# One image's sampling interleaved with the other images' offsets stage, and the whole depthwise convolution as diagonal matmuls

## Chip, cores and metric

The kernel runs on one core of a Trainium2 chip, in float32 throughout. The metric is device time in microseconds. The engines are PE (TensorE matmul; PEld its weight loads), DVE (VectorE), ACT (ScalarE), POOL (GpSimd), and SP, whose queue issues most DMAs.

## The reference

Four images of 64 x 64 positions and 256 channels go through two layers: a deformable convolution (DCNv3 style), and then an additive attention with a routed feed-forward part. Only the first layer touches the change. Cut to what matters:

```python
x1 = lax.conv_general_dilated(x1, dw_k, (1, 1), [(1, 1), (1, 1)], feature_group_count=C)  # depthwise 3x3
x1 = silu(bn(x1))
offset = x1 @ off_w + off_b                       # 8 groups x 9 points x 2
mask = softmax((x1 @ mask_w + mask_b).reshape(N, H, W, G, P), -1)
xp = x @ in_w + in_b                              # the projection that is sampled
# bilinear samples of the padded xp at (position + point + offset), times mask, summed over the 9 points
out = (samples * m).sum(-1) @ out_w + out_b
x = x + out                                       # then attention and feed-forward over the tokens
```

Its input is `_gn(x)`, a group norm with 32 groups over one image, so an image has to be read whole before its convolution can start.

## The kernel before

It works in float32, in these stages, one after the other:

1. `offsets_and_weights` for all four images (called with slabs of 8 token tiles, 8 x 128 tokens, and two row buffers). Per image: `front` loads the image in eight pieces (`xt`), transposes them on PE so that channels lie on partitions, takes statistics on DVE (L332), copies to `xn` on ACT (L333), forms the group statistics through two tiny matmuls, and normalises `xn` in two ACT instructions (L357), one for each half of the channels. Then, slab by slab:
   - `convolution(s)`: the depthwise 3x3. Channel half 1 is nine matmuls with diagonal matrices `diag`, accumulated in PSUM (L411), then SiLU on ACT (L415). Channel half 0 is one multiply and eight multiply-adds on DVE (L423, L425), then SiLU (L426). It is written one slab ahead.
   - `taps(s)`: the matmuls to offsets and mask logits (L435), the bias on DVE into `raw` (L439), the softmax's maximum, subtraction and exponential (L447 to L449).
   - `window(s)`: the softmax's rest, `raw` stored, hat functions of the offsets on ACT (L464 to L468), and from these a 5 x 5 window of weights `w5` for each position and group, built on DVE (L474, L477, L479). It is transposed on PE (L488), copied (L490) and stored to `wt_d` (L492).
   - `projection(i)`: 16 image rows of the sampled projection (L378, L383), stored as rows (`xp_d`, L389) and, transposed (L396, L397), as a table (`tab_d`, L398).

   The `front` of the next image is drawn on between the slabs; `xn` has two buffers.
2. The zero borders of `xp_d` and `tab_d`: one zeroed tile, 24 DMAs on SP (L1306, L1307).
3. `sample_image(0, 6)`: the sampling of image 0 as a dense sum over the 5 x 5 window: for each of 4 chunks of 1024 tokens, 2 channel halves and 25 displacements, a DMA that broadcasts the weights `wb` (L668, 2 x depth buffers), a product on DVE (L677), an accumulation on DVE (L684); then the output projection on PE (L696) with two adds (L700, L703). Ahead of it `list_tokens` lists the tokens whose offsets leave the window, and `exact_rows` does up to 128 of these by gathers (L611, L622, L623), a step of it beside every product.
4. Then for each image the attention, preceded by `attention_prep` (and the feed-forward part of the image before); `sample_image(n + 1)` runs beside the attention of image n. A last feed-forward ends the kernel.

A list scheduler orders the instructions of each engine, in the order of the program where several are ready. `keep(...)` pins an instruction behind everything traced before it on its engine; the products and accumulations of the sampling are pinned. `pinned` is a stand-in for `nc.vector` that pins every instruction. `offsets_and_weights` uses plain `nc.vector`.

Both `offsets_and_weights` and `sample_image` can be generators: the latter yields after every product and every accumulation, which is called a step here.

Of the kernel before, what the change touches and what calls it, by code (L numbers as in the profile page):

```python
# [9 lines left out]
F32 = mybir.dt.float32  # L10
# [6 lines left out]
P = 128  # L17
# [9 lines left out]
MP = 68  # L27
# [17 lines left out]
def layers_kernel(ctx: ExitStack, tc: tile.TileContext, a, out: bass.AP):  # L45
# [208 lines left out]
    def offsets_and_weights(images, slab, rows_bufs):  # L254

        ca = S.a_one
        inw = load_const(ca, "inw", [P, CC, C], a["L0_conv_in_w"].rearrange("(k p) f -> p k f", p=P))
# [50 lines left out]

        diag = ca.tile([P, K2, P], F32, name="diag")
        for tap in range(K2):  # L310
            nc.vector.tensor_scalar(diag[:, tap], ident, dwk[:, 1, tap : tap + 1], None, ALU.mult)

        def front(n):

            xn = S.a_xn.tile([P, CC, PITCH, PITCH], F32, tag="xn", name="xn")
            for k in range(CC):
                for e in (0, PITCH - 1):
                    nc.gpsimd.memset(xn[:, k, e, :], 0.0)
                    nc.gpsimd.memset(xn[:, k, :, e : e + 1], 0.0)

            st = S.a_sm.tile([P, CC, 8, 6], F32, tag="st", name="st")
            for s in range(8):
                xt = S.a_ld.tile([P, 4, C], F32, tag="xt", name="xt")
                nc.sync.dma_start(
                    out=xt, in_=x_d[n, s * 512 : (s + 1) * 512].rearrange("(t p) c -> p t c", p=P)
                )
                for k in range(CC):
                    pt = S.a_t.tile([P, 4, P], F32, tag="pt", name="pt")
                    for t in range(4):
                        nc.tensor.transpose(pt[:, t, :], xt[:, t, k * P : (k + 1) * P], ident)  # L330
                    ptf = pt.rearrange("p t q -> p (t q)")
                    nc.vector.bn_stats(st[:, k, s, :], ptf)  # L332
                    nc.scalar.copy(  # L333
                        xn[:, k, 1 + 8 * s : 9 + 8 * s, 1 : 1 + W],
                        ptf.rearrange("p (r w) -> p r w", w=W),
                    )
                yield
            mv = S.a_sm.tile([P, CC, 2], F32, tag="mv", name="mv")
            for k in range(CC):
                nc.vector.bn_aggr(mv[:, k, :], st[:, k].rearrange("p s f -> p (s f)"))  # L340
# [5 lines left out]
            nc.vector.tensor_copy(gm, pg)  # L346
            gv = S.a_sm.tile([P, CC], F32, tag="gv", name="gv")
            nc.vector.tensor_sub(gv, mv[:, :, 0], gm)
            nc.vector.tensor_mul(gv, gv, gv)
            nc.vector.tensor_add(gv, gv, mv[:, :, 1])  # L350
# [3 lines left out]
            nc.vector.scalar_tensor_tensor(gm, gm, -1.0, gr, ALU.mult, ALU.mult)  # L354
            for k in range(CC):
                inner = xn[:, k, 1 : 1 + H, 1 : 1 + W]
                nc.scalar.activation(inner, inner, AF.Identity, bias=gm[:, k : k + 1], scale=gr[:, k : k + 1])  # L357
            xns[n] = xn

        images = list(images)  # L360
        xns = {}
        for _ in front(images[0]):
            pass
        for at, n in enumerate(images):
            xn = xns.pop(n)
            after = front(images[at + 1]) if at + 1 < len(images) else iter(())


# [34 lines left out]
            def convolution(s):  # L403
                x1 = S.a_wk.tile([P, CC, slab * P], F32, tag="x1", name="x1")
                x1s[s] = x1
                r0 = 2 * slab * s
                for o in range(0, slab * P, 512):
                    pc = S.a_m.tile([P, 8, W], F32, tag="pm", name="pc")
                    for tap in range(K2):
                        r = r0 + o // W + tap // 3  # L410
                        nc.tensor.matmul(  # L411
                            pc, diag[:, tap], xn[:, 1, r : r + 8, tap % 3 : tap % 3 + W],
                            start=(tap == 0), stop=(tap == K2 - 1),
                        )
                    nc.scalar.activation(  # L415
                        x1[:, 1, o : o + 512], pc.rearrange("p r w -> p (r w)"), AF.Silu,
                        bias=bnsh[:, 1:2], scale=bns[:, 1:2],
                    )
                acc = x1[:, 0].rearrange("p (r w) -> p r w", w=W)
                for tap in range(K2):  # L420
                    src = xn[:, 0, r0 + tap // 3 : r0 + tap // 3 + 2 * slab, tap % 3 : tap % 3 + W]
                    if tap == 0:
                        nc.vector.tensor_scalar(acc, src, dwk[:, 0, 0:1], None, ALU.mult)  # L423
                    else:
                        nc.vector.scalar_tensor_tensor(acc, src, dwk[:, 0, tap : tap + 1], acc, ALU.mult, ALU.add)  # L425
                nc.scalar.activation(x1[:, 0], x1[:, 0], AF.Silu, bias=bnsh[:, 0:1], scale=bns[:, 0:1])  # L426

            def taps(s):
                x1 = x1s.pop(s)
                raw = S.a_wk.tile([P, slab, 3 * GP], F32, tag="raw", name="raw")  # L430
                for t in range(0, slab, 2):
                    po = S.a_m.tile([P, 2, 3 * GP], F32, tag="pm", name="po")
                    for j in range(2):
                        for k in range(CC):
# [3 lines left out]
                            )  # L438
                    nc.vector.tensor_tensor(  # L439
                        raw[:, t : t + 2, :], po, omb.to_broadcast([P, 2, 3 * GP]), ALU.add  # L440
# [5 lines left out]
                rbc = red.to_broadcast([P, slab, G, K2])  # L446
                nc.vector.tensor_reduce(red, m3, AX.X, ALU.max)  # L447
                nc.vector.tensor_tensor(m3, m3, rbc, ALU.subtract)
                nc.scalar.activation(m3, m3, AF.Exp)  # L449
                raws[s] = raw, m3, red, rbc  # L450

            def window(s):
                raw, m3, red, rbc = raws.pop(s)
                nc.vector.tensor_reduce(red, m3, AX.X, ALU.add)
                nc.vector.reciprocal(red, red)
                nc.vector.tensor_tensor(m3, m3, rbc, ALU.mult)
                nc.sync.dma_start(
# [8 lines left out]
                nc.scalar.activation(hat[:, 1], off, AF.Abs)  # L466
                nc.vector.tensor_reduce(omax[:, n, s * slab : (s + 1) * slab], hat[:, 1], AX.X, ALU.max)
                nc.scalar.activation(hat[:, 1], hat[:, 1], AF.Identity, scale=-1.0, bias=one_c)  # L468
# [3 lines left out]
                for ey in range(3):  # L472
                    my = S.a_w1p.tile([P, slab, GP], F32, tag="my", name="my", bufs=2)
                    nc.vector.tensor_mul(my, raw[:, :, 2 * GP :], hat[:, ey, :, GP:])  # L474
                    for ex in range(3):
                        mxy = S.a_w1p.tile([P, slab, GP], F32, tag="mxy", name="mxy", bufs=2)
                        nc.vector.tensor_mul(mxy, my, hat[:, ex, :, :GP])  # L477
                        blk = w5[:, :, ex : ex + 3, ey : ey + 3]
                        nc.vector.tensor_tensor(  # L479
                            blk, blk, mxy.rearrange("p t (g i j) -> p (t g) i j", i=3, j=3), ALU.add  # L480
                        )
# [14 lines left out]
            for s in range(ns):  # L496
                if s + 1 < ns:
                    convolution(s + 1)
                taps(s)
                window(s)  # L500
                for i in range(s * (H // 16) // ns, (s + 1) * (H // 16) // ns):
                    projection(i)
                for _ in range(8 // ns):
                    next(after, None)
            for _ in after:
                pass

# [874 lines left out]
```

## Time and profile before

| | us |
|---|---|
| median of 3 runs | 11147.51 (11145.21 to 11148.35) |
| profiled execution, its own time | 11148.32 |
| its span | 11146.6 |
| first `xn` normalised from | 52.8 |
| first product of the sampling (L677) | 872.8 |
| first load of tokens for the attention (L742) | 1478.5 |
| DVE, PE, ACT, POOL busy in the whole span | 8634.7, 9316.6, 7435.1, 5068.5 |

The four images' normalisations begin at 52.8, 247.3, 441.1 and 633.3 us. A row of a group of instructions names the line, the engine, the operation, output and inputs, the tile, the count, the busy time and the mean length of one, then the idle time of that engine just before them and what ended it. Matmuls of float32 operands appear as two records each.

### The profile page before, as it was taken

What the parts mean: (1) busy time and instruction counts of PE and PEld (TensorE: products, weight loads), DVE (VectorE), ACT (ScalarE), POOL (GpSimd) and SP (SyncE); (2) the same over time, 40 slices, a digit from 0 to 9 for tenths busy, and PEclk for the clock granted to TensorE, in tenths of its full rate; (3) what the DMA queues carried; (4) which work ended last, traced back from release to release, by engine and by line L of the source; (5) the groups of instructions that cost most, each with busy time, mean ns of one, the idle gap of its engine ahead of it and who ended that gap; (6) DMA issues with size and microseconds to landing.
All of it is one profiled execution on the core that took longest, in us unless ns stands there. A gap on an engine that the chain in (4) does not pass through costs nothing. (4 is left out here: it accounts for less than half of the span.)

```text
span 11146.6 us, 116484 instructions
## 1 busy us (share of the span) xinstructions
PE 9316.6 (84%) x38460; PEld 4513.2 (40%) x38460; DVE 8634.7 (77%) x13490; ACT 7435.1 (67%) x8505; POOL 5068.5 (45%) x2931
## 2 busy tenths in 40 slices
PE   7870049999999489999999489999999499999994
PEld 4540024444444244444444244444444244444443
DVE  7767859899998549899997459899997447777772
ACT  4440027777888437777888447777888369999982
POOL 0005107754445227654445237654445135555552
PEclk8985559999999789999999689999999699999997
DMA  3336622322220213222220222222220200000002
GB/s 113 121 129 196 216 91 76 69 77 70 74 75 29 76 58 77 70 77 69 71 75 22 82 60 79 68 73 73 71 76 13 86 22 6 9 9 7 6 7 70
DMA packets 381684, 766.42 MB, mean 69 GB/s; under 512 B 49072, under 2 KB 212944, under 8 KB 381040
## 3 DMA queue, kind: packets, MB, share of 16 engines
q1 hardware_dynamic: 350896, 712.74, 19.6%
q0 software_dynamic: 30144, 45.87, 2.9%
q8 instruction: 310, 5.08, 0.2%
q14 instruction: 334, 2.74, 0.1%
HBM read 581.28 MB, written 177.14 MB: 68 GB/s over the span
## 5 line engine op out<-in xcount | busy, mean ns | idle before, releaser
L849 PE MATMUL nn<-qn,kf 32*128 32x512 f32 (+1 forms) x12288 | 4688.4, 653 | 192.6 <-DVE r L854 149.1
L854 DVE TENSOR_TENSOR r<-nn,r 128x512 f32<-128x512 f32 x6144 | 3946.3, 683 | 952.5 <-PE nn L849 925.4
L926 POOL TENSOR_TENSOR r<-r 128x1024 f32<-128x1024 f32 x1024 | 2721.3, 2658 | 3191.7 <-DVE r L854 3161.0
L920 ACT ACTIVATE r<-d 128x1024 f32<-128x1024 f32 x3072 | 3116.8, 1015 | 1411.9 <-DVE r L930 917.9
L839 PE MATMUL d<-qf,kf 32*128 32x512 f32 (+1 forms) x12288 | 3404.6, 642 | 51.1 <-ACT r L920 49.9
L922 ACT ACTIVATE r<-r 128x1024 f32<-128x1024 f32 x3072 | 3123.9, 1051 | 32.7
L849 PEld LDWEIGHTS nn<-qn,kf 32*128 32x128 f32 (+1 forms) x12288 | 1444.9, 187 | 2057.5 <-DVE r L854 1645.9
L876 PE MATMUL pv<-v,et 128*128 128x257 f32 x8192 | 2203.2, 414 | 14.7 <-DVE acv L896 14.7
L876 PEld LDWEIGHTS pv<-v,et 128*128 128x128 f32 x8192 | 1576.7, 203 | 1047.6 <-issue 815.6
L839 PEld LDWEIGHTS d<-qf,kf 32*128 32x128 f32 (+1 forms) x12288 | 1027.7, 188 | 1316.3 <-issue 575.2
L928 POOL TENSOR_TENSOR r<-r 128x512 f32<-128x512 f32 x1024 | 1321.4, 1290 | 94.7 <-DVE r L854 16.4
L684 DVE TENSOR_TENSOR ac<-ac,prd 128x1024 f32<-128x1024 f32 x768 | 1008.9, 1314 | 6.2
L677 DVE TENSOR_TENSOR prd<-xs,wb 128x1024 f32<-128x1024 f32 x768 | 980.9, 1277 | 0.0
L611 POOL DMA_INDIRECT ga<-tab,tii x576 | 742.8, 1290 | 240.0 <-issue 121.6
L860 ACT ACTIVATE et<-et,nshift 128x512 f32<-128x512 f32 x1024 | 723.6, 707 | 26.6 <-DVE et L933 26.6
L930 DVE TENSOR_TENSOR r<-r 128x512 f32<-128x512 f32 x1024 | 707.9, 691 | 12.5 <-POOL r L926 12.1
L933 DVE TENSOR_TENSOR et<-r 128x512 f32<-128x512 f32 x1024 | 697.3, 681 | 5.5 <-POOL r L928 5.0
L110 ACT ACT_TABLE_LOAD x9 | 11.5, 1283 | 888.4 <-DVE mv L738 730.0
L696 PE MATMUL pmo<-outwp,ac 128*128 128x256 f32 x512 | 141.4, 427 | 455.3 <-DVE ac L684 407.6
L1239 POOL DMA_INDIRECT sort<-v,rif x128 | 123.0, 961 | 517.3 <-DVE rif L250 360.8
L1131 PE MATMUL pcn<-kpart,ones 128*128 128x15 f32 (+2 forms) x72 | 21.6, 378 | 396.0 <-DVE kjunk L250 212.1
L471 POOL MEMSET w<- 128x1600 f32 x16 | 22.9, 1432 | 678.1 <-PE ptw L488 481.9
(347 smaller groups left out, 5496.1 us busy)
## 6 DMA issues: line engine op xcount, KB each, us to landing
wb<-wt SPq DMA_DIRECT2D x800, 512.0 KB
tab<-tb SPq DMA_DIRECT2D x128, 256.0 KB
v<-t SPq DMA_DIRECT2D x64, 512.0 KB
xs<-xp SPq DMA_DIRECT2D x32, 680.0 KB
xp<-xp SPq DMA_DIRECT2D x32, 544.0 KB
xt<-in_x_dram SPq DMA_DIRECT2D x32, 512.0 KB
xr<-in_x_dram SPq DMA_DIRECT2D x64, 256.0 KB
t<-xr SPq DMA_DIRECT2D x64, 256.0 KB
```

The costliest lines, as they stand in the source:

```text
L611: keep(nc.gpsimd.indirect_dma_start(out=ga[:, s, dy].rearrange("p c e -> p (c e)"), out_offset=None, in_=tab_d[n], in_offset=bass.Indirect ...
L677: keep(nc.vector.tensor_tensor(pr.rearrange("p (r w) -> p r w", w=W), src, wb.rearrange("p (r w) -> p r w", w=W), ALU.mult,))
L684: keep(nc.vector.tensor_add(ac[:, f, :], ac[:, f, :], pr))
L839: keep(nc.tensor.matmul(d[:, j, :], kf[g, blk, rows(kt)], qs[q][0][g, blk, :], start=True, stop=True))
L849: keep(nc.tensor.matmul(nn, kf[g, blk, rows(kt)], qs[q][1][g, blk, :], start=True, stop=True))
L854: keep(nc.vector.tensor_tensor(r[:, j, :], ns[j], r[:, j, :], ALU.mult))
L860: keep(nc.scalar.activation(ets[b], ets[b], AF.Exp, bias=nshift))
L876: keep(nc.tensor.matmul(pv, ets[b0 + i][:, rows(j)], v[:, k0 + i, :], start=(i == 0), stop=(i == PVB - 1)))
L920: keep(nc.scalar.activation(rs[b, p], ds.pop((b, p)), AF.Ln))
L922: keep(nc.scalar.activation(rs[b, p], rs[b, p], AF.Exp, scale=-1.0))
L926: keep(nc.gpsimd.tensor_tensor(rs[b, 1], rs[b, 1], rs[b, 2], ALU.add))
L928: keep(nc.gpsimd.tensor_tensor(rs[b, 1][:, 0], rs[b, 1][:, 0], rs[b, 3][:, 0], ALU.add))
```

## The change

- The zero borders move ahead of everything else and are issued from ACT's queue.
- `offsets_and_weights` becomes a generator with slabs of 4 token tiles instead of 8, one row buffer, one `xn` buffer and fewer `xt`, `tb`, `wT` and PSUM buffers. It runs image 0 by itself up to its first yield. Then the other three images are worked through with their DVE instructions pinned, yielding after each of eight loading steps, after each `taps` and after each slab's `window` and projections, and at each of these yields six steps of `sample_image(0, 2)` are drawn. `sample_image` has a depth of 2 in place of 6: four `wb` buffers in place of twelve, two of the others as before.
- An image's `front` is no longer drawn on beside the slabs of the image before it, but ahead of its own slabs.
- The depthwise convolution of both channel halves is done by diagonal matmuls; `diag` has 18 matrices in place of 9, and L423, L425 and L426 go.

The diff, cut to its core; `vec.` replaces `nc.vector.` in all of `front`, `taps` and `window` in the same manner as in the lines shown:

```diff
-        diag = ca.tile([P, K2, P], F32, name="diag")
-        for tap in range(K2):
-            nc.vector.tensor_scalar(diag[:, tap], ident, dwk[:, 1, tap : tap + 1], None, ALU.mult)
-
-        def front(n):
+        diag = ca.tile([P, CC, K2, P], F32, name="diag")
+        for k in range(CC):
+            for tap in range(K2):
+                nc.vector.tensor_scalar(diag[:, k, tap], ident, dwk[:, k, tap : tap + 1], None, ALU.mult)
+
+        def front(n, vec):
...
-                    nc.vector.bn_stats(st[:, k, s, :], ptf)
+                    vec.bn_stats(st[:, k, s, :], ptf)
...
-        for _ in front(images[0]):
-            pass
-        for at, n in enumerate(images):
+        for n in images:
+            first = n == images[0]
+            vec = nc.vector if first else pinned
+            for _ in front(n, vec):
+                if not first:
+                    yield
             xn = xns.pop(n)
-            after = front(images[at + 1]) if at + 1 < len(images) else iter(())
...
-                for o in range(0, slab * P, 512):
-                    pc = S.a_m.tile([P, 8, W], F32, tag="pm", name="pc")
-                    for tap in range(K2):
-                        r = r0 + o // W + tap // 3
-                        nc.tensor.matmul(
-                            pc, diag[:, tap], xn[:, 1, r : r + 8, tap % 3 : tap % 3 + W],
-                            start=(tap == 0), stop=(tap == K2 - 1),
+                for k in range(CC):
+                    for o in range(0, slab * P, 512):
+                        pc = S.a_m.tile([P, 8, W], F32, tag="pm", name="pc")
+                        for tap in range(K2):
+                            r = r0 + o // W + tap // 3
+                            nc.tensor.matmul(
+                                pc, diag[:, k, tap], xn[:, k, r : r + 8, tap % 3 : tap % 3 + W],
+                                start=(tap == 0), stop=(tap == K2 - 1),
+                            )
+                        nc.scalar.activation(
+                            x1[:, k, o : o + 512], pc.rearrange("p r w -> p (r w)"), AF.Silu,
+                            bias=bnsh[:, k : k + 1], scale=bns[:, k : k + 1],
                         )
...
-                acc = x1[:, 0].rearrange("p (r w) -> p r w", w=W)
-                for tap in range(K2):
-                    src = xn[:, 0, r0 + tap // 3 : r0 + tap // 3 + 2 * slab, tap % 3 : tap % 3 + W]
-                    if tap == 0:
-                        nc.vector.tensor_scalar(acc, src, dwk[:, 0, 0:1], None, ALU.mult)
-                    else:
-                        nc.vector.scalar_tensor_tensor(acc, src, dwk[:, 0, tap : tap + 1], acc, ALU.mult, ALU.add)
-                nc.scalar.activation(x1[:, 0], x1[:, 0], AF.Silu, bias=bnsh[:, 0:1], scale=bns[:, 0:1])
...
                 taps(s)
+                if not first:
+                    yield
                 window(s)
                 for i in range(s * (H // 16) // ns, (s + 1) * (H // 16) // ns):
                     projection(i)
-                for _ in range(8 // ns):
-                    next(after, None)
-            for _ in after:
-                pass
+                if not first:
+                    yield
+            if first:
+                yield
...
-    with scope(
-        ("a_one", 1, 0), ("a_xn", 2, 0), ("a_ld", 3, 0), ("a_wk", 2, 0), ("a_w1p", 1, 0), ("a_sm", 2, 0),
-        ("a_t", 4, 1), ("a_m", 4, 1),
-    ):
-        offsets_and_weights(range(NB), SLAB, 2)
...
-                    nc.sync.dma_start(out=xp_d[n][f][:, q0 : q0 + 2 * MP], in_=zm[:, : 2 * MP])
-                nc.sync.dma_start(
+                    nc.scalar.dma_start(out=xp_d[n][f][:, q0 : q0 + 2 * MP], in_=zm[:, : 2 * MP])
+                nc.scalar.dma_start(
                     out=tabw[q0 : q0 + 2 * MP].rearrange("(p r) c -> p (r c)", r=2), in_=zm[:MP]
                 )
...
-    with scope(("two", 2, 0), ("sb", 2, 0), ("dn", 1, 0), ("ps_m", 2, 1)):
-        for _ in sample_image(0, 6):
+    with scope(
+        ("a_one", 1, 0), ("a_xn", 1, 0), ("a_ld", 2, 0), ("a_wk", 2, 0), ("a_w1p", 1, 0), ("a_sm", 2, 0),
+        ("two", 2, 0), ("sb", 2, 0), ("dn", 1, 0), ("a_t", 3, 1), ("a_m", 3, 1), ("ps_m", 2, 1),
+    ):
+        others = offsets_and_weights(range(NB), SLAB // 2, 1)
+        next(others)
+        first = sample_image(0, 2)
+        for _ in others:
+            for _ in range(6):
+                next(first, None)
+        for _ in first:
             pass
```

More of the change, by code (lines that the diff above doesn't have):

```diff
@@ L339, in front @@
             for k in range(CC):
-                nc.vector.bn_aggr(mv[:, k, :], st[:, k].rearrange("p s f -> p (s f)"))
+                vec.bn_aggr(mv[:, k, :], st[:, k].rearrange("p s f -> p (s f)"))
             gavgf = gavg.rearrange("p a b -> p (a b)")
@@ L345, in front @@
             gm = S.a_sm.tile([P, CC], F32, tag="gm", name="gm")
-            nc.vector.tensor_copy(gm, pg)
+            vec.tensor_copy(gm, pg)
             gv = S.a_sm.tile([P, CC], F32, tag="gv", name="gv")
-            nc.vector.tensor_sub(gv, mv[:, :, 0], gm)
-            nc.vector.tensor_mul(gv, gv, gv)
-            nc.vector.tensor_add(gv, gv, mv[:, :, 1])
+            vec.tensor_sub(gv, mv[:, :, 0], gm)
+            vec.tensor_mul(gv, gv, gv)
+            vec.tensor_add(gv, gv, mv[:, :, 1])
             pg2 = S.a_t.tile([P, CC], F32, tag="pt", name="pg2")
@@ L353, in front @@
             gr = inv_std(S.a_sm, pg2, CC, "gr")
-            nc.vector.scalar_tensor_tensor(gm, gm, -1.0, gr, ALU.mult, ALU.mult)
+            vec.scalar_tensor_tensor(gm, gm, -1.0, gr, ALU.mult, ALU.mult)
             for k in range(CC):
@@ L406, in convolution @@
                 r0 = 2 * slab * s
-                for o in range(0, slab * P, 512):
-                    pc = S.a_m.tile([P, 8, W], F32, tag="pm", name="pc")
-                    for tap in range(K2):
-                        r = r0 + o // W + tap // 3
-                        nc.tensor.matmul(
-                            pc, diag[:, tap], xn[:, 1, r : r + 8, tap % 3 : tap % 3 + W],
-                            start=(tap == 0), stop=(tap == K2 - 1),
-                        )
[L415 to L418, printed above, removed]
-                acc = x1[:, 0].rearrange("p (r w) -> p r w", w=W)
-                for tap in range(K2):
-                    src = xn[:, 0, r0 + tap // 3 : r0 + tap // 3 + 2 * slab, tap % 3 : tap % 3 + W]
-                    if tap == 0:
-                        nc.vector.tensor_scalar(acc, src, dwk[:, 0, 0:1], None, ALU.mult)
-                    else:
-                        nc.vector.scalar_tensor_tensor(acc, src, dwk[:, 0, tap : tap + 1], acc, ALU.mult, ALU.add)
-                nc.scalar.activation(x1[:, 0], x1[:, 0], AF.Silu, bias=bnsh[:, 0:1], scale=bns[:, 0:1])
+                for k in range(CC):
[10 more added lines that the diff above has]
+                            bias=bnsh[:, k : k + 1], scale=bns[:, k : k + 1],
+                        )
             def taps(s):
@@ L438, in taps @@
                             )
-                    nc.vector.tensor_tensor(
+                    vec.tensor_tensor(
                         raw[:, t : t + 2, :], po, omb.to_broadcast([P, 2, 3 * GP]), ALU.add
@@ L446, in taps @@
                 rbc = red.to_broadcast([P, slab, G, K2])
-                nc.vector.tensor_reduce(red, m3, AX.X, ALU.max)
-                nc.vector.tensor_tensor(m3, m3, rbc, ALU.subtract)
+                vec.tensor_reduce(red, m3, AX.X, ALU.max)
+                vec.tensor_tensor(m3, m3, rbc, ALU.subtract)
                 nc.scalar.activation(m3, m3, AF.Exp)
@@ L453, in window @@
                 raw, m3, red, rbc = raws.pop(s)
-                nc.vector.tensor_reduce(red, m3, AX.X, ALU.add)
-                nc.vector.reciprocal(red, red)
-                nc.vector.tensor_tensor(m3, m3, rbc, ALU.mult)
+                vec.tensor_reduce(red, m3, AX.X, ALU.add)
+                vec.reciprocal(red, red)
+                vec.tensor_tensor(m3, m3, rbc, ALU.mult)
                 nc.sync.dma_start(
@@ L466, in window @@
                 nc.scalar.activation(hat[:, 1], off, AF.Abs)
-                nc.vector.tensor_reduce(omax[:, n, s * slab : (s + 1) * slab], hat[:, 1], AX.X, ALU.max)
+                vec.tensor_reduce(omax[:, n, s * slab : (s + 1) * slab], hat[:, 1], AX.X, ALU.max)
                 nc.scalar.activation(hat[:, 1], hat[:, 1], AF.Identity, scale=-1.0, bias=one_c)
@@ L473, in window @@
                     my = S.a_w1p.tile([P, slab, GP], F32, tag="my", name="my", bufs=2)
-                    nc.vector.tensor_mul(my, raw[:, :, 2 * GP :], hat[:, ey, :, GP:])
+                    vec.tensor_mul(my, raw[:, :, 2 * GP :], hat[:, ey, :, GP:])
                     for ex in range(3):
                         mxy = S.a_w1p.tile([P, slab, GP], F32, tag="mxy", name="mxy", bufs=2)
-                        nc.vector.tensor_mul(mxy, my, hat[:, ex, :, :GP])
+                        vec.tensor_mul(mxy, my, hat[:, ex, :, :GP])
                         blk = w5[:, :, ex : ex + 3, ey : ey + 3]
-                        nc.vector.tensor_tensor(
+                        vec.tensor_tensor(
                             blk, blk, mxy.rearrange("p t (g i j) -> p (t g) i j", i=3, j=3), ALU.add
```

## The prediction

> **What bounds the kernel now.** I first read the slices of the page, then the busy time by stretch of everything ahead of the first attention, then that stretch's groups by line, then the order of time around one image's start. First the slices (tenths busy, a slice is 279 us; the third row is the granted TensorE clock), then the stretches (start:end, length, then busy PE, PEld, DVE, ACT, POOL, clock, DMA share, GB/s): two of the offsets stage, and six from its end through image 0's sampling.
>
> ```profile
> PE   7870049999999489999999489999999499999994
> DVE  7767859899998549899997459899997447777772
> PEclk8985559999999789999999689999999699999997
> ```
> ```profile
> 240.00:430.00 190.00, 155.60 (x606) 92.68 (x604) 138.00 (x184) 94.82 (x160) 6.78 (x12) 0.92 0.37 127
> 430.00:620.00 190.00, 158.65 (x606) 96.58 (x604) 138.61 (x184) 94.55 (x158) 5.73 (x4) 0.89 0.36 122
> ...
> 815.00:852.00 37.00, 0.00 (x0) 0.00 (x0) 0.00 (x0) 0.00 (x1) 0.67 (x1) 0.50 0.43 128
> 852.00:873.00 21.00, 16.55 (x68) 15.76 (x68) 12.46 (x55) 0.00 (x0) 0.00 (x0) 0.50 0.70 277
> 873.00:1000.00 127.00, 2.07 (x4) 1.17 (x4) 103.65 (x109) 0.00 (x0) 78.56 (x61) 0.50 0.68 187
> 1000.00:1180.00 180.00, 8.73 (x29) 6.80 (x29) 150.38 (x128) 0.00 (x0) 110.61 (x86) 0.52 0.74 205
> 1180.00:1460.00 280.00, 26.91 (x76) 19.68 (x77) 257.13 (x226) 0.00 (x0) 0.00 (x0) 0.52 0.59 195
> 1460.00:1480.00 20.00, 6.94 (x27) 5.54 (x25) 4.89 (x8) 0.00 (x0) 1.16 (x2) 0.67 0.30 87
> ```
> To be seen: the first stage (to 815 us) takes 190 us an image and is PE's (156 of 190), with DVE at 138. Then 37 us of nothing but zero fills, then 626 us in which DVE alone works (528 us over the six rows) while PE does 61. Two stages with complementary needs stand one behind the other. The attention of the first image cannot be prepared before that: its first load of tokens is issued at 1478.5 us. Everything after 1478.5 the change leaves as it is, so I predict that one point.
>
> One image's groups, 241 to 431 us (count | busy us, mean ns | idle before):
> ```profile
> L411 PE MATMUL pc<-xn,diag 128*128 128x512 f32 x144 | 66.4, 615 | 8.3 <-ACT xn L357 8.3
> L425 DVE SCALAR_TENSOR_TENSOR x<-xn,dwk,x 128x1024 f32<-128x1024 f32 x32 | 40.9, 1279 | 0.7
> L423 DVE TENSOR_SCALAR x<-xn,dwk 128x1024 f32<-128x1024 f32 x4 | 3.0, 751 | 3.9 <-ACT xn L357 3.9
> L378 PE MATMUL pm<-xn,inwp 128*128 128x512 f32 x64 | 32.1, 623 | 4.9 <-DVE raw L439 4.9
> ```
> The half convolution on DVE costs 43.9 us an image, the other half on PE 66.4.
>
> And the order of time at an image's start (start, length, x is the count):
> ```profile
> 52.77 7.50 ACT L357 ACTIVATE xn<-xn,gm,gr 128x4096 f32<-128x4096 f32 x2 [0.49 <-DVE gm L354]
> 60.33 34.18 PE L411 MATMUL pc<-xn,diag 128*128 128x512 f32 x72 [8.34 <-ACT xn L357]
> 94.34 6.00 PE L435 MATMUL po<-wom,x 128*128 128x216 f32 x32
> ```
> To be seen: PE runs the convolutions of slab 0 and of slab 1 (72 records, two for each float32 matmul) before the first offsets matmul, though slab 0's half was done after 36.
>
> **What the Trainium skill says.** "PSUM — Partial Sum Buffer", section "Engine vs sequencer instructions": VectorE's queue is strict FIFO. That is what pinning costs: a pinned instruction that waits holds all sampling behind it. The trace agrees: at 879.75 us one DVE wait of 4.93 us for gathered rows stopped DVE, though products behind it had their data. "TensorE: Matmul & The Clock Gate", section "What's actually happening": an idle array falls to half its clock and needs some 3.4 us of activity to come back. Here the weight loads from 60.33 to 66.4 us come 0.86 us apart and then 0.43: a price of 3 us for each idle start. "DMA: Bandwidth & Descriptors", section "Issuing engines are not separate DMA queues": issuing from another engine saves only that sequencer's issue time. No row here has ACT issuing a DMA.
>
> **The change part by part.** Span 11146.6 us; that run took 11148.32, the median is 11147.51.
>
> *Zero fills moved to the start, issued by ACT.* At the old place they and the drain ahead of them cost 852 − 815 = 37 us; gone there. At the start they need memory which the first constants also use, free at about 27 us (the load of inw is issued at 27.48). 24 issues took SP 31 us (815.7 to 845.3). On ACT they queue with the copies of the first image (9.4 us), needed by 49 us. If all of it stood in the way, 25 us; if the issues are hidden, 0. I take 10.
>
> *Image 0's offsets alone.* PE per image: 157 busy (of 156 to 159) plus 66 for the second channel half = 223; less the 10 us of loading transposes that lie ahead of the normalisation, 213. Start 52.8 + 3.9 (first half normalised) + 3 (clock) + 213 + 10 of idle (beside the 8.3 for xn, an image lost some 25 us of 190; with a freer DVE, less) = 282 us. With the zero fills 292.
>
> *DVE per image.* 138 − 44 = 94. Slabs of 4 instead of 8 turn 104 instructions (184 less 36 convolution, 16 statistics, 16 of raw, which keep their number, and 12 small) into 208. Rows of 128x512 and 128x256 take 690 and 426 ns: 1.03 ns an element and 162 fixed; neighbours overlap by some 90 (1.43 us for two of 0.756). So 7 to 17 us, I take 11: 105. All three images: 315.
>
> *Sampling of image 0.* 528 us of DVE (sum of the six rows above). It is now handed out six steps at a time; a product or an accumulation is one step, 1.2 us (2.40 a pair). There are 1 + 4 × (98 + 4) = 409 steps; 8 + 16 turns an image times 3 images = 72 turns, 432 steps: it lasts until three turns before the end. So DVE has 528 + 315 = 843 us of work in this stage and PE 3 × 223 + 61 = 730.
>
> *In order, per image* (DVE is pinned; PE, ACT and SP are not):
> - Loading, 8 turns: 8 × (1.3 of statistics + 7.2 of sampling) = 68, and 5 because one xn buffer makes the copies wait for the last projection of the image before. PE has little to do here.
> - A gap with nothing to sample in it: from the last statistics through the normalisation, both first convolutions and the first offsets matmul to raw. The next DVE instruction in program order is the add to raw. Aggregation 2.9 (244.35 to 247.23), first half normalised 3.9, 72 records × 0.43 = 31, clock 3, first offsets 1: 41 us. DVE stands still for nearly all of it. If PE took the offsets of slab 0 ahead of slab 1's convolution, 15 less; the order above says it doesn't.
> - Eight slabs. DVE: (105 − 13)/8 + 12 × 1.2 = 25.9 us. PE: 213/8 = 26.6. They are almost equal, so neither has slack and every mismatch is paid. In the offsets stage PE was busy 156 of 190 us, i.e. a loss of 22% of its work, 8.3 us of it counted above. With PE free to run ahead I take 15%: 30.5 us a slab, 244 in all. Both ends: 26.6 (none lost) and 36 (35% lost).
>
> Sum per image 73 + 41 + 244 = 358; three 1074. Listing tokens comes first, 21 us (852 to 873), and the end needs 10 us of drain. 292 + 21 + 1074 + 10 = 1397 against 1478.5: 81 us earlier. 11147 − 81 = **11066 us**.
>
> *Edits with one answer.* Fewer buffers (xt, tb 2 instead of 3, three PSUM buffers for transposes and matmuls instead of four): ACT has 95 us of work in 190 and empties them in time; hidden by PE's own work, up to 2 us a slab if not, inside the 15%. Nine more diagonals: 9 × 0.28 us on DVE in the start-up. More exponent and SiLU table loads, 1.28 us each, some ten an image on ACT: hidden by the same slack. DMA: 95 MB × 3/4 + 123 MB in some 1090 us is 178 GB/s, under the 195 to 205 that the sampling alone drew.
>
> **The rivals.**
> 1. *Nearly ideal overlap* (0.22). PE runs ahead through the spare x1 and raw buffers and a slab costs 26.6. For it: the scheduler already interleaves projections between waits. Against: 22% lost today. 24 × 3.9 = 94 us better: 10972.
> 2. *Late weights* (0.10). SP issues a projection's 11 stores (3.3 MB, 12 us at 277 GB/s) ahead of the sampling's weight loads, which have four buffers instead of twelve. A wait of 7 us in each of 12 projections returns 84 us: 11150, no change. For it: waits on ACT's copies fill SP's list (251 us for xp). Against: three loads a turn and four buffers, so most are there before the turn.
> 3. *The other side: PE in the order of the text* (0.20). DVE, in order, cannot add raw of slab s+1 before PE's offsets; PE cannot run them if it waits first for window s's transposes and has the convolution of s+2 behind these. Then a slab is raw 1.9 + samples 7.2 + window 9.8 + transposes 1.2 + convolution 16.5 + offsets 1.5 = 38 us, 7.5 over mine: 24 × 7.5 = 180 us, 11246. It decides from 33.9 us a slab on (81/24 = 3.4 over mine). For it: PE waited 39 us in all for the window in the first stage, up to 10.7 at once. Against: there the next convolution does run ahead of the window's transposes (107 and 131 us).
>
> **The numbers.** Forecast 0.48, rivals 0.22, 0.10, 0.20. A measurement can tell about 0.2%, 22 us. Faster: forecast and rival 1 nearly whole = 0.68; same, from rival 2 and the forecast's upper edge, 0.10; slower 0.22. The forecast's own range is 11010 to 11130 (28.2 to 33.2 us a slab); rival 1 with no start-up cost gives 10960, and rival 3 in most slabs 11210: 10955 to 11210.
>
> **What would show it.** Right: no zero fills ahead of the first product, which starts near 310 us; no L425; three gaps of about 40 us on DVE that end with PE's offsets; attention's first load near 1397. Wrong: DVE waits for PE's offsets in every slab over 5 us (rival 3), waits of products for wb (rival 2), or the first image's stage ending after 310 us.

## The result and the profile after

The changed kernel takes 11128.19 us (median), the kernel before 11150.46 in the same runs: 22 us less, a ratio of 0.998 with a 95% interval of 0.9973 to 0.9987. The forecast was 81 us less. The span of the profiled execution is 11132.4 us.

The slices of the page after (PE and DVE busy in tenths, then PE's granted clock):

```profile
PE   6658769999999489999999489999999499999994
DVE  3777749899998549899997459899997347777772
PEclk9779869999999689999999689999999699999997
```

PE's work now lies across the first five slices instead of the first three, and DVE is at 7 tenths in slices 2 to 5, where it was at 6 to 8. The stretches of the stage (columns as before) are image 0 by itself, then images 1, 2 and 3 beside the sampling, each from the end of the slabs of the one before it (for image 1 from the end of the listing of tokens, at 343 us), and what is left at the end:

```profile
96.50:322.00 225.50, 203.47 (x663) 109.69 (x664) 99.10 (x252) 97.73 (x160) 7.17 (x16) 0.95 0.27 94
343.00:728.50 385.50, 244.32 (x767) 132.63 (x765) 300.77 (x431) 111.50 (x183) 128.61 (x125) 0.80 0.60 174
728.50:1101.60 373.10, 246.03 (x797) 135.20 (x797) 292.63 (x412) 115.52 (x194) 54.80 (x52) 0.81 0.56 181
1101.60:1437.00 335.40, 242.84 (x794) 134.54 (x794) 255.43 (x386) 112.94 (x188) 5.90 (x7) 0.84 0.50 168
1437.00:1459.30 22.30, 11.59 (x44) 6.90 (x44) 0.00 (x0) 7.56 (x20) 0.00 (x0) 0.58 0.34 119
```

Image 0 by itself is PE's (203 of 225 us). Beside the sampling neither engine is full: DVE is busy in 301 of 385 us, PE in 244. The first load of tokens for the attention is issued at 1459.3 us, where it was 1478.5: 19 us earlier. The medians differ by 22 us and the two profiled executions by 14, so the result lies ahead of this point.

Three places show where much of the overlap's gain went. First, the start, in order of time (start, length, what; ACTq and SPq are DMA issues):

```profile
25.85 0.95 POOL L1297 MEMSET zm<- 128x1024 f32 x1 [0.56 <-DVE slotr L218]
26.83 0.83 ACTq L1302 DMA_DIRECT2D xp<-zm  x2
...
53.85 2.44 ACTq L1303 DMA_DIRECT2D tab<-zm  x1
62.26 0.39 SPq L68 DMA_DIRECT2D inw<-in_L_conv_in_w_dram  x1
62.28 0.20 POOL L299 MEMSET gavg<- 128x128 f32 x1 [35.48 <-DMA tab<-zm]
...
65.59 0.68 DVE L263 COPY inwp<-inw 128x256 f32<-128x256 f32 x2 [39.80 <-DMA womr<-in_L_conv_off_w_dram]
...
96.53 3.81 ACT L361 ACTIVATE xn<-xn,gm,gr 128x4096 f32<-128x4096 f32 x1 [0.49 <-DVE gm L358]
```

The zeroed tile sits in a scope of its own, and the stage's scope is given the same memory after it. So the load of the first constant waits on SP until the last fill has landed (62.26 us; it was 27.48 before), POOL waits 35.5 us for the same, and the first normalisation begins at 96.5 us instead of 52.8.

Second, each image's gap, and third, the wait ahead of its first statistics. These are DVE's longest waits while images 1 to 3 are worked through beside the sampling; a fourth, of 12.6 us, stands ahead of image 3's statistics. The ACT and PE rows lead to the statistics at 743.93:

```profile
469.77 0.61 DVE L250 TENSOR_TENSOR raw<-po,omb 128x432 f32<-128x432 f32 x1 [38.19 <-PE po L434]
...
743.93 0.70 DVE L250 BATCH_NORM_STATS2 st<-pt 128x6 f32<-128x512 f32 x1 [15.45 <-PE pt L334]
...
868.35 0.61 DVE L250 TENSOR_TENSOR raw<-po,omb 128x432 f32<-128x432 f32 x1 [38.39 <-PE po L434]
...
1233.07 0.61 DVE L250 TENSOR_TENSOR raw<-po,omb 128x432 f32<-128x432 f32 x1 [39.45 <-PE po L434]
```
```profile
721.44 1.92 PE L487 MATMUL ptw<-ident,w 128*100 128x128 f32 x8 [26.16 <-DVE w L250]
723.15 3.32 PE L402 MATMUL ptc<-ident,xp 128*128 128x128 f32 x14
...
737.11 0.37 ACT L403 COPY tb<-ptc 128x256 f32<-128x256 f32 x1 [5.09 <-DMA tab<-tb]
737.54 0.69 PE L402 MATMUL ptc<-ident,xp 128*128 128x128 f32 x2 [4.78 <-ACT tb L403]
...
742.35 0.90 PE L334 MATMUL pt<-ident,xt 128*128 128x128 f32 x3 [0.46 <-ACT tb L403]
```

DVE stands still for 38 to 39 us at each of the three images between its normalisation and its first `raw`. At 743.93 the statistics wait for PE's loading transposes, which stand on PE behind the transposes of the last projection's table; these wait for ACT to copy into `tb`, and ACT for an earlier store out of `tb`. The table's transposes in turn began only at 723.15, after PE had waited 26 us for DVE's last window. Such a wait is not new. The kernel before had it too, with three `tb` and two `xn` buffers:

```profile
431.83 0.70 DVE L332 BATCH_NORM_STATS2 st<-pt 128x6 f32<-128x512 f32 x1 [13.46 <-PE pt L330]
```

The stage's groups (from 0 to 1450 us) carry the parts (L250 is the line of the pinned operations):

```profile
L418 PE MATMUL pc<-xn,diag 128*128 128x512 f32 x1152 | 521.1, 600 | 19.0 <-ACT xn L361 17.2 <-ACT xp L389 1.6 <-issue 0.2
L403 ACT COPY tb<-ptc 128x256 f32<-128x256 f32 (+1 forms) x282 | 98.3, 373 | 182.1 <-DMA tab<-tb 108.6 <-PE ptc L402 58.5 <-issue 7.0
L250 DVE TENSOR_TENSOR raw<-po,omb 128x432 f32<-128x432 f32 x48 | 27.1, 601 | 118.6 <-PE po L434 118.6
L678 DVE TENSOR_TENSOR prd<-xs,wb 128x1024 f32<-128x1024 f32 x192 | 234.1, 1219 | 3.7 <-DMA wb<-wt 3.7
```

The multiply-adds of the convolution are gone from DVE and PE's half has doubled (264 us before, 521 now). The last row says that the products waited for their weights 3.7 us in all. The third row says that apart from the three gaps (116 us of its 118.6) DVE hardly waited for PE's offsets in images 1 to 3.

The same stage by part (columns as before), first the three loadings up to the normalisation, then the slabs of the three images from the first `raw`:

```profile
343.00:431.67 88.67, 17.33 (x68) 12.76 (x66) 76.35 (x93) 11.94 (x21) 47.92 (x40) 0.50 0.74 218
728.50:830.06 101.56, 27.62 (x98) 18.58 (x99) 78.27 (x80) 15.84 (x33) 47.64 (x36) 0.50 0.71 217
1101.60:1193.72 92.12, 33.08 (x118) 23.78 (x118) 68.22 (x77) 15.80 (x33) 0.00 (x0) 0.54 0.66 224
...
469.77:728.50 258.73, 192.85 (x619) 103.86 (x617) 224.42 (x338) 87.66 (x155) 66.55 (x70) 0.89 0.60 183
868.35:1101.60 233.25, 183.16 (x618) 100.47 (x616) 214.36 (x332) 87.78 (x155) 7.16 (x16) 0.92 0.59 194
1233.07:1437.00 203.93, 174.37 (x596) 94.31 (x594) 187.22 (x309) 85.24 (x149) 5.90 (x7) 0.97 0.53 175
```

DVE stands still for 60 us of the loadings and for 70 us of the slabs; in the slabs it is busier than PE.

### The profile page after: what moved, and what is told of

The parts are those of the page before. It is cut to its first block, busy times and chain, and to the rows that moved or that the text cites. A ratio compares the mean times of both kernels' runs of the same rounds, so it can differ in the third digit from the quotient of the medians.

```text
span 11132.4 us, 118179 instructions
## 1 busy us (share of the span) xinstructions
PE 9608.4 (86%) x39036; PEld 4632.7 (42%) x39036; DVE 8522.7 (77%) x13787; ACT 7510.5 (67%) x8633; POOL 5047.8 (45%) x2946
## 5 line engine op out<-in xcount | busy, mean ns | idle before, releaser
L861 ACT ACTIVATE et<-et,nshift 128x512 f32<-128x512 f32 x1024 | 723.4, 706 | 26.6 <-DVE et L934 26.6
L931 DVE TENSOR_TENSOR r<-r 128x512 f32<-128x512 f32 x1024 | 709.3, 693 | 12.5 <-POOL r L927 12.1
L418 PE MATMUL pc<-xn,diag 128*128 128x512 f32 x1152 | 521.1, 600 | 19.0 <-ACT xn L361 17.2
L470 POOL MEMSET w<- 128x800 f32 x32 | 24.5, 766 | 939.1 <-PE ptw L487 875.8
L418 PEld LDWEIGHTS pc<-xn,diag 128*128 128x128 f32 x1152 | 214.0, 192 | 256.8 <-issue 244.4
```

The source lines that it names most:

```text
L418: nc.tensor.matmul(pc, diag[:, k, tap], xn[:, k, r : r + 8, tap % 3 : tap % 3 + W], start=(tap == 0), stop=(tap == K2 - 1),)
```

## The experiments

The theory: the overlap works, and four losses pay its gain back, which are the fills at the start, the gaps, the wait at the loading, and PE's second half of the convolution in image 0, which has no one beside it. Times are medians, to be held against 11128.19. The experiments ran at other times than the changed kernel: the kernel before took 11147 to 11148 us beside them and 11150.46 beside it, so a difference of 3 us says nothing.

**1. The zeroed tile in memory of its own.** Edit:

```diff
-    with scope(("one", 1, 0)):
-        zm = S.one.tile([P, 2 * G * 2 * CG], F32, name="zm")
...
+        zm = S.a_one.tile([P, 2 * G * 2 * CG], F32, name="zm")
```

> The changed kernel with one edit: the zeroed tile lies in the pool of the stage's constants instead of in a scope of its own, so nothing has to wait for it to be given back; the 24 fills stay first and on ACT's queue. Theory (the constants' loads and all that follows wait for the memory of the zeroed tile, given back when the last fill has landed): the loads of the constants are issued near 27 us instead of 62, the first normalisation starts at 60 to 70 us instead of 96.5, the time falls by 25 to 37 us to 11091 to 11103. Rival (ACT's queue holds the copies of the first image behind 30 us of issues, whatever the memory): the normalisation starts at 85 us or later and the time falls by under 12 us.

Measured: 11103.43 us, 25 less (ratio to before 0.996, 0.9946 to 0.9974). The constants' loads are issued from 25.84 us. But the normalisation still begins only at 84.0. In order of time:

```profile
26.81 0.85 ACTq L1307 DMA_DIRECT2D xp<-zm  x2
...
58.17 0.91 ACTq L1308 DMA_DIRECT2D tab<-zm  x1
59.12 1.28 ACT L110 ACT_TABLE_LOAD   x1 [47.34 <-DMA xp<-zm]
...
60.61 1.54 ACT L337 COPY xn<-pt 128x512 f32<-128x512 f32 x3
61.23 2.82 PE L334 MATMUL pt<-ident,xt 128*128 128x128 f32 x12 [29.00 <-ACT xn L337]
```

Both mechanisms are real: with the memory free, ACT's queue is what is left. It issues fills until 59 us, and the copies of the first image stand behind them; PE waits 29 us for these. The normalisation comes later than the theory allowed and just ahead of the rival's 85 us. The fall in time is just short of the theory's 25 to 37 us, but of the normalisation's 44 us only 12.5 came back, so the time is not carried by the start alone: another 10 us were gained between the normalisations of images 1 and 2, in several small waits, and their cause stays open. The start is settled by experiment 5.

**2. Sampling traced into the gaps.** Edit (the driver draws as many steps as are yielded):

```diff
             for _ in front(n, vec):
                 if not first:
-                    yield
+                    yield 3
...
                 if s + 1 < ns:
                     convolution(s + 1)
+                if not first and s == 0:
+                    yield 24
                 taps(s)
```

> The changed kernel with the turns handed out otherwise: 3 steps of sampling instead of 6 at each of the eight loading turns, and the 24 that this frees between the first two convolutions of an image and its first add to raw. Theory (in the three gaps of 38 to 39 us DVE stands still only because nothing is traced there): the gaps shrink to 10 us or less, the time falls by 80 to 95 us to about 11040. Rival A (the loading turns, with half their sampling, are then held by their own chain of transposes, statistics and copies): the gaps shrink, but the loading grows, and the time falls by 30 to 50 us. Rival B (SP's order brings the weights too late in the gap): waits of products for wb of over 20 us per image, and the time falls by under 30 us.

Measured: 11020.03 us, 108 less (ratio to before 0.9881, 0.9864 to 0.9897). The gaps' ends now:

```profile
435.85 0.61 DVE L250 TENSOR_TENSOR raw<-po,omb 128x432 f32<-128x432 f32 x1 [5.75 <-PE po L434]
...
790.39 0.61 DVE L250 TENSOR_TENSOR raw<-po,omb 128x432 f32<-128x432 f32 x1 [7.35 <-PE po L434]
...
1125.74 0.61 DVE L250 TENSOR_TENSOR raw<-po,omb 128x432 f32<-128x432 f32 x1 [9.82 <-PE po L434]
```

The three waits fell from 116 us to 23, which accounts for 93 of the 108. From normalisation to first `raw` it still takes 38 to 39 us, but DVE now samples there, and the loadings, with half their steps, are some 36, 37 and 30 us shorter; image 1's slabs are 8 us shorter for a reason I did not follow. The gain is more than expected, and both rivals fall: the loadings did not grow, and no product waited for its weights.

**3. The fills first, in the kernel before.** The only edit is the change's own, the fills moved ahead and issued by ACT.

> The kernel before with one part of the change: the zero fills first and on ACT's queue. Theory (at their new place they cost what they saved at the old one): first normalisation at 95 to 97 us instead of 52.8, sampling's first product 6 to 12 us later than before, time 11150 to 11165. Rival (the late start comes from something else of the change, such as fewer buffers or 18 diagonals): normalisation at 53 to 70 us, time 11115 to 11130.

Measured: 11153.71 us (1.0005, 0.9997 to 1.0014): no difference. The first normalisation begins at 87.4 us (52.8 before), less late than the 95 to 97 expected; the attention's first load comes at 1472.2 (1478.5 before). So the fills take back at the start 35 us, which leaves 6 of the 41 that they set free at the end, and the remaining 9 us of the changed kernel's late start belong to other edits or to their company with the fills.

**4. Both halves by diagonal matmuls, in the kernel before.** The only edit is the change's `diag` and `convolution`.

> The kernel before with one part of the change: both channel halves of the depthwise convolution by diagonal matmuls. Theory (the stage is PE's, and the second half costs what the first does, 66 us of PE an image): an image's period grows from 194 to 250 to 262 us, the time by 225 to 270 us to about 11395. Rival (DVE's 44 us set free an image take away most of PE's idle time): the period grows to 230 to 240, the time to about 11310.

Measured: 11407.93 us, 260 more (1.0232, 1.0215 to 1.0249). One image:

```profile
54.00:312.00 258.00, 225.23 (x756) 126.64 (x756) 98.16 (x146) 98.98 (x165) 6.83 (x12) 0.91 0.28 94
```

PE's 225 us of work take 258, where 156 took 190: with nothing but this stage to do, the second half costs its full 66 us an image, as expected. In the change image 0 is in this position.

**5. The fills by image, on SP's queue, behind that image's loads.** The zeroed tile lies among the stage's constants, and the fills ahead of the stage go. Edit, in the image's own part of `offsets_and_weights`:

```diff
             tabw = tab_d[n].rearrange("(q g) c -> q (g c)", g=G)
+            for q0 in (0, (H + 2) * MP):
+                for f in range(CC):
+                    keep(nc.sync.dma_start(out=xp_d[n][f][:, q0 : q0 + 2 * MP], in_=zm[:, : 2 * MP]))
+                keep(nc.sync.dma_start(
+                    out=tabw[q0 : q0 + 2 * MP].rearrange("(p r) c -> p (r c)", r=2), in_=zm[:MP]
+                ))
```

> The changed kernel with the zero fills split by image and moved: those of image n follow that image's loads on SP's queue, from a tile in the pool of the constants. Theory (the fills cost what they hold up at the start, through memory and through ACT's queue, and nothing where neither waits for them): first normalisation at 53 to 60 us instead of 96.5, the time falls by 35 to 45 us to about 11088. Rival (18 diagonals and fewer buffers hold the start as well): normalisation at 70 us or later, the time falls by under 27 us.

Measured: 11084.84 us, 43 less (ratio to before 0.9946, 0.9929 to 0.9963). The first normalisation, by its line:

```profile
L361 ACT ACTIVATE xn<-xn,gm,gr x2: 3791/3802/3812, 58.1 to 61.8; 128x4096 f32<-128x4096 f32 x2
```

It begins at 58.1 us, 38 earlier. The fills cost nothing that shows in their new place, and nearly all of the late start was theirs; the 5 us that remain were not followed.

**6. The edits of experiments 2 and 5 together.**

> The last two edits together: fills by image on SP's queue, and 24 steps of sampling traced in each gap. Theory (start and gaps are separate losses and add up): 11020 less 35 to 45 us, about 10980. Rival (with the gaps filled DMA or PE is what the stage waits for, and the earlier start is lost again): above 11005.

Measured: 10987.90 us (0.9856, 0.984 to 0.9872), 32 less than experiment 2 alone. They add up, less about 11 us, a little short of the 35 to 45 expected.

**7. The projections one slab earlier**, upon experiment 6. Edit:

```diff
-                for i in range(s * (H // 16) // ns, (s + 1) * (H // 16) // ns):
-                    projection(i)
+                if s % 2 == 0:
+                    projection(s // 2)
```

> The same, and each projection one slab earlier (after slabs 0, 2, 4, 6 instead of 1, 3, 5, 7), so that the last reader of xn is done a slab sooner. Theory (the waits of 12 to 15 us at the first loading turn of images 2 and 3 are for the single xn buffer, held by the last projection): these waits go, the time falls by 20 to 30 us below the run without this edit. Rival (they are PE's order: the loading's transposes queue behind other work): the waits stay and the time changes by under 8 us.

Measured: 10947.47 us (0.9821, 0.9804 to 0.9837), 40 less than experiment 6, more than expected. The waits of 13.6 and 12.5 us at the first statistics are gone, and the wait of DVE's first instruction after the stage, for the last table stores, fell from 22.2 to 8.9 us: 39 of the 40 us. The two rows are experiment 6, then this one:

```profile
1322.68 0.14 DVE L821 TENSOR_SCALAR lo<-top 1x1 f32<-1x1 f32 x1 [22.15 <-DMA tab<-tb]
...
1275.59 0.14 DVE L821 TENSOR_SCALAR lo<-top 1x1 f32<-1x1 f32 x1 [8.92 <-DMA tab<-tb]
```

The experiment alone does not tell `xn`'s single buffer from PE's order, since an earlier projection mends both. The trace of the changed kernel does. The last matmuls of the projection that read image 1's `xn`, and the first writes into the buffer for image 2, come well ahead of the wait, which ran from 728.5 to 743.9 us; for image 3 the first write, held by the projection's last matmuls, came at 1064.10, and the slabs went on to 1101.6:

```profile
689.59 3.78 PE L384 MATMUL pm<-xn,inwp 128*128 128x512 f32 x4 [0.57 <-ACT xp L389]
...
702.95 0.26 POOL L322 MEMSET xn<- 128x66 f32 x2
...
1064.10 0.24 POOL L322 MEMSET xn<- 128x66 f32 x2 [22.28 <-PE pm L384]
```

So the buffer was free both times, and the wait was PE's order: its loading transposes stood behind the table's, which waited for `tb`. That is the rival's mechanism with the theory's gain.

**8. One half on DVE again, for all images.** The edit takes the `diag` and `convolution` of before, with the pinned DVE.

> The changed kernel with one part undone: channel half 0 of the convolution on DVE again (pinned for images 1 to 3), half 1 by diagonal matmuls. Theory (in this stage DVE is the longer one, so 44 us more of it an image cost more than PE's 66 save; but a part lies in the gaps, which get shorter, and image 0's stage is PE's): gaps with 11 us of DVE work in them and 26 to 28 us long, image 0 30 to 40 us shorter, the other three 15 to 30 longer each, time 11130 to 11190. Rival A (all of it shows): three times 44 more less 35, about 11225. Rival B (PE bounds the stage): faster, under 11110.

Measured: 11160.00 us (1.0011, 1.0004 to 1.0017), 32 more than the changed kernel, as expected. Image 0, from its normalisation to the sampling's first product, takes 186 us instead of 243, which is 57 less where 30 to 40 were expected, and a gap's last wait is short because DVE convolves in it:

```profile
397.95 0.61 DVE L250 TENSOR_TENSOR raw<-po,omb 128x432 f32<-128x432 f32 x1 [8.89 <-PE po L440]
```

So in images 1 to 3 the whole convolution on PE is worth some 90 us (32 + 57), and 57 of these are lost in image 0. Both rivals fall.

**9. One half on DVE for image 0 alone**, upon experiment 7. Edit:

```diff
-                for k in range(CC):
+                for k in range(1 if first else 0, CC):
...
+                if first:
+                    acc = x1[:, 0].rearrange("p (r w) -> p r w", w=W)
...
```

> The fills by image, the gaps filled and the projections earlier, as in the run before, and for image 0 alone the half convolution on DVE as in the kernel of before. Theory (image 0's stage, with nothing to share it, is PE's: 208 us busy of 220, DVE 100; 66 us of PE less and 44 of DVE more make it shorter, and the three others stay as they are): image 0's stage, from its normalisation to the first product of the sampling, 35 to 45 us shorter, time about 10908. Rival (the end of image 0's stage is a chain of the last slab through DVE and the listing, which a busier DVE makes longer): under 20 us, time above 10927.

Measured: 10898.49 us (0.9776, 0.976 to 0.9792), 49 less than experiment 7, a little more than expected. The sampling's first product comes at 250.3 us instead of 298.5. From the normalisation up to there, in experiment 7 and then here:

```profile
57.00:298.50 241.50, 226.66 (x776) 131.87 (x776) 109.48 (x289) 104.00 (x178) 7.21 (x16) 0.92 0.30 106
...
57.00:250.30 193.30, 167.15 (x632) 104.00 (x632) 151.99 (x361) 103.07 (x178) 7.21 (x16) 0.90 0.38 132
```

PE's work fell by 60 us, DVE's grew by 43, and the stretch is 48 shorter: DVE's added work went into time in which it had waited for PE (for offsets, 99 us in experiment 7 and 18 here). This version is 249 us faster than the kernel before in the same runs (11147.35) and 230 faster than the changed one.

## Why the prediction was right in direction and wrong in size

The overlap is there, the first load of the attention comes earlier, and the time falls. But two terms of the sum had their mechanism wrong, the start and the loading, and the first load comes 62 us later than forecast. By the terms of the prediction's sum:

| term | predicted | measured | difference |
|---|---|---|---|
| first normalisation | 62.8 | 96.5 | +34 |
| image 0 from there to the listing | 229 | 225.5 | −4 |
| listing | 21 | 21 | 0 |
| loading with aggregation, three images | 228 | 282 | +54 |
| normalisation to `raw`, three images | 114 | 116 | +2 |
| slabs, three images | 732 | 696 | −36 |
| drain | 10 | 22 | +12 |
| attention's first load | 1397 | 1459.3 | +62 |

- **The first step that failed** is "Zero fills moved to the start, issued by ACT ... I take 10". The start came 44 us later, outside the term's own bounds of 0 to 25, and experiment 5 gives 38 of these back. I had named the shared memory and ACT's queue, but priced only how long the issues take (and wrote 31 us for SP's, which took 29.6). What counted was that everything with that memory waits for the *landing* of the last fill, and that the loading of the first image then runs after the fills instead of beside them. Experiment 1 shows both parts, and experiment 3 that the fills alone take back most of what they had set free.
- **The second step that failed, and the larger one,** is the loading: "8 × (1.3 of statistics + 7.2 of sampling) = 68, and 5 because one xn buffer makes the copies wait". It took 18 us an image more. A little of it is work: a step was priced at 1.2 us, a bare product or accumulation, but the steps also carry the gathers' products and reductions and the adds of the output projection, 1.26 us each (528 us less the listing's 12, over 409 steps). DVE was busy 223 us in the three loadings where I had 213, the aggregation included. The rest is waits, 60 us where I had 15. Of these, 15.4 and 12.6 us stand ahead of the first statistics of images 2 and 3, some 15 belong to the gathered rows, and some 8 to the output projection. The reason I gave was wrong: `xn`'s buffer was free (experiment 7), and PE's order held the transposes back. The trace of the kernel before showed such a wait, of 13.46 us, where I priced 5. Of the fewer buffers I wrote "hidden by PE's own work"; ACT's copies into the two `tb` buffers waited 108.6 us for the stores, where three buffers had waited 25.4. Whether the buffers or the busier DMA made this difference was not tested.
- **The gap was right**: 38 to 39 us after the normalisation, for the reason given, the order of two convolutions ahead of the first offsets. Experiment 2 confirms it by filling it with sampling.
- **Image 0 by itself was right** (225.5 against 229), and so was PE's full price for the second half (experiment 4: 225 us of PE an image against 223).
- **The slabs came out 36 us cheaper, and that was luck.** I had counted the two convolutions that PE does in each gap (PE is busy 34 to 35 us there) once in the gap and again in PE's 213 us of the slabs. So PE had slack where I saw none, and DVE set the pace. In images 1 and 2 a slab took 32.3 and 29.2 us, on the mean 30.7 where I had 30.5, but for another reason: DVE had 27.4 us of work in it instead of 25.9, and waited little for PE. In image 3 it took 25.5: the sampling ran out there, as the prediction says, but its price charges all 432 steps where there are 409. The 23 missing steps at 1.2 us are 28 of the 36 us; without this offset the forecast would have missed by so much more.
- **No rival came true.** Nearly ideal overlap asked for 26.6 us a slab, and the images with a full share of sampling took more. Late weights: 3.7 us. PE in the order of the text: apart from the gaps, 2.6 us of waits for offsets in all three images. The forecast's own sign of being wrong did come true: the first image's stage ended at 322 us, after 310.
- The drain was 22 us, since the last projection's transposes and stores come after everything else; moving the projections (experiment 7) cut it.

The Trainium skill's place on VectorE's queue ("PSUM — Partial Sum Buffer", "Engine vs sequencer instructions") carried the right step, the gaps: DVE was busy for 0.00 us from 431.67 to 469.77 us, with sampling behind the waiting instruction. The place in "DMA: Bandwidth & Descriptors", "Issuing engines are not separate DMA queues", fits in that the fills took as long to issue from ACT as from SP (29.5 and 29.6 us), but its remark that the time to initiate a DMA is usually small does not fit these fills. Of the clock, where "TensorE: Matmul & The Clock Gate", "What's actually happening", speaks of some 3.4 us, the traces show from 3.3 us at half rate (435.60 to 438.92 in the changed kernel) to 6.1 us (60.33 to 66.4 in the kernel before).

## What to carry to other kernels

When two stages are interleaved by hand, look for the stretches of the one in which it has nothing for the shared engine, and trace the other stage's work exactly there: here 24 of 144 steps an image, moved from where PE had nothing to do to where DVE had nothing to do, were worth 108 us. Work that is moved "to the start" is not free because the start is idle: price what shares its memory and its queue until it has landed. And moving work from one engine to another paid here only in the stretches where the first had other work to take up (some 90 us in images 1 to 3); where the stage ran alone it cost 57 us.

## What had not been expected of the hardware

- The 24 fills (3.3 MB) took 29.5 us to issue on ACT (26.8 to 56.3) and 29.6 us on SP in the kernel before (815.7 to 845.3): the queue of issue made no difference. A fill of 68 KB held ACT's queue for 0.80 us at the median, up to 2.1, and one of 272 KB for 1.64, up to 2.5, while a weight load of 512 KB held SP's for 0.51. In experiment 5, with six at a time, the same two kinds of fill held SP's queue for 0.45 and 0.44 us at the median, some 19 us for all 24. So neither their size nor their shape sets it; that it is their number in a row was not tested. An engine that has copies to do behind such issues stands still: in experiment 1, ACT's first copies came at 60.61 us, and PE waited 29 us for them.
- From the last fill's issue to the first instruction that its landing set free passed another 6 us (56.3 to 62.26).
